# Attention scores issued three head pairs at a time, with one merged exponential behind each projection or feed-forward piece

## The chip, the cores and the metric

The kernel runs on one core of one Trainium2 chip. The metric is the device time of one execution in microseconds; the profile's span runs from the first to the last instruction of the profiled execution. Engines are named as the profile names them: PE (TensorE matmuls), PEld (its weight loads), DVE (VectorE), ACT (ScalarE), POOL (GpSimd), SP (SyncE, whose queue issues the DMAs).

## The reference

A batch of 16 graphs of 1024 nodes with 128 features goes through three graph transformer layers and one graph attention layer; one adjacency matrix (about 1.6% of ones) is shared by all.

```
layer (three times, x of 16 x 1024 x 128, 8 heads of 16):
  Q, K, V = x Wq, x Wk, x Wv
  attn    = softmax over m of (Q K^T / 4, with -inf where adj[n, m] == 0)
  x       = layer_norm(x + attn V Wo + bo)
  x       = layer_norm(x + relu(x W1 + b1) W2 + b2)
last layer (once, one head of 128):
  h   = x W
  e   = leaky_relu(h a_src [i] + h a_dst [j], 0.2), -inf where adj[i, j] == 0
  out = layer_norm(softmax over j of e, times h, plus x)
```

Everything is in float32. The kernel's ordinary path is `fast_path`; `general_path` stands behind a check at the end and isn't run with these inputs.

## The kernel before, in words

The work is cut into 48 blocks, one for each graph and layer, in groups of four graphs (`LANES`): layer 0 of graphs 0 to 3, layer 1 of the same, and so on. A block has 32 attention steps: two groups of four heads (`g`), two halves of 512 queries (`qh`), eight tiles of 128 keys (`kt`). A step has two head pairs (`pp`). In the first and last block the halves are the outer loop. Scores are held transposed: keys on the partitions, queries along the row.

For a head pair, PE makes two score matmuls that share the array by rows (64 rows each; L423) into one PSUM slot of 128 x 1024 from `slot()`. There are three such slots. The pair is then masked in one of two ways. On the DVE way, DVE adds a mask of 0 or a large negative number while it copies the pair to SBUF (L433), and ACT takes the exponential there in place (L445). On the POOL way, ACT takes the exponential on its way out of PSUM (L430), and POOL multiplies by a mask of 0 or 1 (L431). The POOL way is taken by the first pair of a step, except for `kt` in `BOTH_ON_DVE`, so by 5 of 16 pairs. Four steps later (`AHEAD`), `av_due` issues the step's four attention-value products (L450; float32, so eight records in the profile), which share the array by columns and add up in the single PSUM bank `acc`, with the row sums as a seventeenth column. After eight steps the half is finished: `finish` has DVE transpose `acc` to `tt` (L461), and POOL scales it (L464).

The rest of a block's work is cut into pieces held in queues (`chains`). After each step `piece()` takes at most one piece that is due. `proj` pieces make the next block's inputs: two transposes (`t0`), the splits of K and Q into high and low float32r parts (`split`; ACT writes `hi`, L385, DVE writes `lo`, L386), and V. `post` pieces end a block: transposes of the attention result (L477), the output projection, residual addition (L329), layer norm statistics on DVE (L322, L324), `normalise` on POOL (L337 to L341), the feed-forward halves. `last` pieces are the graph attention layer, of which `edges` fills two slots and has DVE turn them into weights (L610), and `aggregate` multiplies these with the nodes. Matmul pieces share the array by columns (L297); transposes take the whole array (L286). Except at both ends of the kernel, all pieces use one PSUM bank, `t`, with one buffer.

When a piece is due is set by a table of steps in its block (`AT`, and `AT_END` near the end) or, for `last`, by distances in steps. The orders of PE and ACT are as written (`manual_schedule`); the orders of DVE, POOL and SP come from a scheduler, in which operations inside `soon()` stand earlier. `stack` copies the split K and Q parts into the row layout of the scores by 32 DMAs from SP for each group of heads. SBUF tiles for exponentials come from `e_tile()`: six buffers of 128 x 4 x 512.

## Time and profile before

| what | value |
|---|---|
| median of 3 runs | 3982.76 us (3978.65 to 3982.88) |
| profiled execution, its own time | 3983.09 us |
| its span | 3981.2 us |
| mean granted PE clock | 0.987 of full speed |
| busy: PE, DVE, ACT, POOL | 3758.5, 3408.3, 3392.8, 3331.4 us |
| HBM traffic | 6 GB/s over the span |

Busy time is that in which at least one instruction of the engine is open. The groups give, for a line and shape, the count, the busy time, the mean duration of one, and the engine's idle time just ahead of it with what ended that. The timeline gives start, duration, engine and line, and merges neighbours of one line ("x4"); a bracket holds idle time and what ended it. The chain follows the work that ended last back through what released each part. Ends of matmuls are modelled, so distances from start to start tell more than durations.

### The profile page before, as it was taken

Reading aid. Unit: us, or ns where it says so; the run is one execution under the profiler, and the core shown is the slowest. Engines: PE = TensorE matmul, PEld = TensorE weight load, DVE = VectorE, ACT = ScalarE, POOL = GpSimd, SP = SyncE. Lnnn points to the kernel's source line nnn. Section 1 sums busy time; section 2 is a strip of 40 time slices with the busy share of each in tenths; the row PEclk is TensorE's granted clock in tenths of the full one; section 3 lists DMA queues with packets and bytes.
Section 4 is the critical chain, followed back from the end, with each engine's and each line's share of the span. In section 5 each row is a group of like instructions: output and inputs, shape, how many; then the busy total and the mean of one; then the engine's idle time right before and its main releaser. Section 6 shows DMA issues by size and latency. Waiting matters only on the chain.

```text
span 3981.2 us, 107823 instructions
## 1 busy us (share of the span) xinstructions
PE 3758.5 (94%) x44501; PEld 1558.5 (39%) x44501; DVE 3408.3 (86%) x5326; ACT 3392.8 (85%) x3961; POOL 3331.4 (84%) x3010
## 2 busy tenths in 40 slices
PE   7999999999999999999999999999999999999996
PEld 2333333344443333334444333333444433333345
DVE  7888988988888988988888898888888898898874
ACT  7999999977779999997777999999777799999860
POOL 4788888987789888988778888888877898898875
PEclk8999999999999999999999999999999999999998
DMA  6222222112222222222222222221222212222200
GB/s 163 65 65 53 55 65 63 46 48 65 56 58 57 65 65 54 54 65 55 55 55 55 65 53 56 65 64 45 55 55 55 71 46 62 65 51 58 66 8 20
DMA packets 124465, 233.13 MB, mean 59 GB/s; under 512 B 34624, under 2 KB 73792, under 8 KB 123968
## 3 DMA queue, kind: packets, MB, share of 16 engines
q1 hardware_dynamic: 123056, 225.74, 22.5%
q8 instruction: 354, 5.80, 0.6%
q14 instruction: 143, 1.17, 0.1%
q10 hardware_dynamic: 912, 0.42, 0.0%
HBM read 15.54 MB, written 8.39 MB: 6 GB/s over the span
## 4 chain that ended last, share of the span: by engine, by line
PE 61%; DVE 22%; POOL 9%; ACT 4%; issue 3%; SPq 0%; DMA 0%; DVEq 0%; ACTq 0%; POOLq 0%
PE acc L450 23%; PE t L297 19%; PE s L423 16%; DVE e L433 13%; POOL e L431 3%; POOL x L341 2%; PE t L286 2%; DVE lo L386 2%; DVE st L322 2%; ACT e L445 2%; ACT e L430 2%; DVE tt L461 1%; POOL mv L339 1%; PE s L297 1%; POOL x L345 1%
## 5 line engine op out<-in xcount | busy, mean ns | idle before, releaser
L433 DVE TENSOR_TENSOR e<-s,mask_add 128x1024 f32<-128x1024 f32 x2112 | 2493.6, 1213 | 344.6 <-PE s L423 263.7
L445 ACT ACTIVATE e<-e 128x1024 f32<-128x1024 f32 x2112 | 2203.4, 1060 | 206.1 <-DVE e L433 187.9
L431 POOL TENSOR_TENSOR e<-e,mask 128x1024 f32<-128x1024 f32 x960 | 1933.5, 2026 | 419.0 <-ACT e L430 419.0
L450 PE MATMUL acc<-e,v 128*17 128x512 f32 x12288 | 1627.8, 601 | 73.3 <-DVE tt L461 47.8
L423 PE MATMUL s<-Wq,Wk 64*128 64x512 f32 x6144 | 1185.0, 456 | 58.1 <-DVE e L433 41.3
L430 ACT ACTIVATE e<-s 128x1024 f32<-128x1024 f32 x960 | 980.8, 1022 | 227.5 <-PE s L423 226.5
L423 PEld LDWEIGHTS s<-Wq,Wk 64*128 64x128 f32 x6144 | 501.2, 185 | 1027.9 <-DVE e L433 417.1
L450 PEld LDWEIGHTS acc<-e,v 128*17 128x17 f32 x12288 | 208.6, 95 | 582.1 <-issue 452.0
L341 POOL TENSOR_SCALAR x<-x,mv 128x128 f32<-128x128 f32 x896 | 389.1, 447 | 23.5
L345 POOL TENSOR_TENSOR x<-x,ln_g 128x1024 f32<-128x1024 f32 (+1 forms) x97 | 229.5, 2367 | 25.1 <-PE t L286 22.6
L339 POOL TENSOR_TENSOR mv<-mv,half_neg 128x4 f32<-128x4 f32 x224 | 232.4, 1038 | 18.6
L297 PE MATMUL t<-hd,e 128*32 128x129 f32 x7040 | 208.2, 275 | 1.2
L329 DVE TENSOR_TENSOR x<-t,x 128x512 f32<-128x512 f32 x191 | 130.8, 685 | 86.9 <-PE t L297 86.9
L297 PEld LDWEIGHTS t<-hd,e 128*32 128x32 f32 x7040 | 194.6, 110 | 16.0 <-issue 5.0
L322 DVE BATCH_NORM_STATS2 st<-x 128x6 f32<-128x128 f32 x896 | 197.3, 280 | 3.3
L297 PE MATMUL t<-x1T,W 128*32 128x512 f32 x1520 | 198.0, 592 | 0.0
L297 PEld LDWEIGHTS t<-W,hT 128*32 128x32 f32 x6080 | 170.0, 110 | 58.5 <-issue 45.5
L297 PE MATMUL t<-W,hT 128*32 128x128 f32 x6080 | 183.4, 273 | 0.2 <-DVE x L625 0.2
L286 PE MATMUL t<-identf,x 128*128 128x128 f32 x872 | 151.0, 289 | 34.0 <-DVE lo L386 15.4
L286 PEld LDWEIGHTS t<-identf,x 128*128 128x128 f32 x872 | 92.9, 141 | 230.2 <-issue 108.3
L337 POOL TENSOR_SCALAR mv<-mv 128x4 f32<-128x4 f32 x224 | 53.0, 236 | 124.6 <-DVE mv L324 98.8
L610 DVE SCALAR_TENSOR_TENSOR e<-s,mask 128x1024 f32<-128x1024 f32 x128 | 150.3, 1214 | 5.9 <-PE s L607 5.0
(118 smaller groups left out, 2573.9 us busy)
## 6 DMA issues: line engine op xcount, KB each, us to landing
Wk<-hi SPq DMA_DIRECT2D x384, 128.0 KB
Wk<-lo SPq DMA_DIRECT2D x384, 128.0 KB
Wq<-hi SPq DMA_DIRECT2D x384, 128.0 KB
Wq<-lo SPq DMA_DIRECT2D x384, 128.0 KB
x<-in_x_dram SPq DMA_DIRECT2D x16, 512.0 KB
out_dram<-x SPq DMA_DIRECT2D x31, 256.0 KB
ai<-in_adj_dram SPq DMA_DIRECT2D x8, 512.0 KB
g_rows<-parts SPq DMA_DIRECT2D x124, 4.0 KB
```

The costliest lines, as they stand in the source:

```text
L286: nc.tensor.transpose(ps[:, t * P:(t + 1) * P], src[:, 4 * h + t, :], identf)
L297: nc.tensor.matmul(dst[j:j + SLOT, :], lhsT[:, j:j + SLOT], rhs, start=start, stop=stop)
L322: nc.vector.bn_stats(st[:, t, :], z[:, t, :])
L339: nc.gpsimd.tensor_tensor(v, v, half_neg[:, ts], OP.pow)
L341: nc.gpsimd.tensor_scalar(z[:, t, :], z[:, t, :], mv[:, t, 0:1], mv[:, t, 1:2], op0=OP.add, op1=OP.mult)
L345: nc.gpsimd.tensor_mul(z, z, rows(gain, n))
L423: nc.tensor.matmul(ps[:, r * 512:(r + 1) * 512], k[64 * r:64 * r + 64, kt * P:(kt + 1) * P], q[64 * r:64 * r + 64, q0:q0 + 512], start=Tru ...
L430: nc.scalar.activation(ev, psv, AF.Exp, scale=HD ** -0.5)
L431: behind["pool"] = nc.gpsimd.tensor_mul(ev, ev, m).ins
L433: behind["dve"] = nc.vector.tensor_add(ev, psv, m).ins
L445: nc.scalar.activation(ev, ev, AF.Exp, scale=HD ** -0.5)
L450: nc.tensor.matmul(acc[j * SLOT:j * SLOT + HD + 1, :], v_bufs[m % 2][:, kt, 2 * j + g, :], e[:, j, :], start=first, stop=last)
```

## The change

Score work is no longer issued by the step but in bursts. A burst is three head pairs in a row (one step and a half), each with its own slot. Its second pair goes the POOL way and the two others the DVE way; every sixteenth burst (`POOL_RESTS`) leaves POOL out. The two DVE pairs of a burst lie side by side in one tile (`e_tile`, five buffers), so that one exponential of 128 x 2048 covers both; the other pair has a tile of its own (`e_pair`, four buffers). The exponential of a burst is issued in the next burst. After the scores of a burst the loop takes one piece if one is due, then issues the exponentials of the burst before, then the attention-value products of the steps that were complete three bursts ago (`AHEAD`), then looks for a piece once more. If two steps are due and the first is the last of its half, that one goes ahead of the piece. The filling of edges becomes a job of its own (`extra`): it takes the place of two pairs in a burst, whose one pair goes the POOL way. The due times lie at multiples of one and a half steps; the K and Q splits alternate; the transposes of the second half come after the first half's feed-forward pieces; `two` now takes its second function first. The last four row blocks of the mask are built in the first four bursts instead of steps 1 to 4.

```diff
-FIRST = 1
-
-
-AT = {"proj": (3, 6, 9, 11, 14, 17, 19, 20), "post": (12, 22, 23, 25, 26, 27, 28, 30, 32, 40, 41)}
-AT_END = {3: (12, 21, 22, 24, 25, 26, 27, 28, 30, 31), 2: (8, 9, 13, 14, 15, 16, 17, 18, 20, 21)}
-AHEAD = 4
-BOTH_ON_DVE = (2, 5, 7)
+
+
+AT = {"proj": (1.5, 4.5, 9, 10.5, 12, 15, 16.5, 18), "post": (13.5, 19.5, 21, 22.5, 24, 25.5, 27, 28.5, 30, 39.5)}
+AT_END = {3: (13.5, 19.5, 21, 22.5, 24, 25.5, 27, 28.5, 30, 31.5), 2: (7.5, 9, 12, 13.5, 15, 16.5, 18, 19.5, 21, 22.5)}
+AHEAD = 3
+BURST = 3
+POOL_RESTS = 16
+E_TILES = {"e": 5, "ep": 4}
...
-        return work.tile([P, J, 512], F32, tag="e", name="e", bufs=6)
+        return work.tile([P, J, 512], F32, tag="e", name="e", bufs=E_TILES["e"])
+
+    def e_pair():
+        return work.tile([P, 2, 512], F32, tag="ep", name="e", bufs=E_TILES["ep"])
...
-        pieces = [t0(0), t0(1), split("Wk", 0), split("Wk", 1), split("Wq", 0), split("Wq", 1), v(0), v(1)]
+        pieces = [t0(0), t0(1), split("Wk", 0), split("Wq", 0), split("Wk", 1), split("Wq", 1), v(0), v(1)]
...
-    def score_step(step):
+    def scores(step, pp):
+
         m, g, qh, kt = step
-        e = e_tile()
-        q0 = qh * 512
-        for pp in range(2):
-            q, k = state["Wq", g, pp], state["Wk", g, pp]
-            ps = slot()
-            for r in range(2):
-                nc.tensor.matmul(ps[:, r * 512:(r + 1) * 512], k[64 * r:64 * r + 64, kt * P:(kt + 1) * P],
-                                 q[64 * r:64 * r + 64, q0:q0 + 512], start=True, stop=True)
-            ev = e[:, 2 * pp:2 * pp + 2, :]
-            psv = ps.rearrange("p (r q) -> p r q", q=512)
-            on_pool = pp == 0 and kt not in BOTH_ON_DVE
-            m = (mask01 if on_pool else mask_add)[:, kt, q0:q0 + 512][:, None, :].to_broadcast([P, 2, 512])
-            if on_pool:
-                nc.scalar.activation(ev, psv, AF.Exp, scale=HD ** -0.5)
-                behind["pool"] = nc.gpsimd.tensor_mul(ev, ev, m).ins
-            else:
-                behind["dve"] = nc.vector.tensor_add(ev, psv, m).ins
-                masked.append((2 * step_no[0] + pp + (kt not in BOTH_ON_DVE), ev))
-        step_no[0] += 1
-        exponentials()
-        return e
-
-    masked, step_no = [], [0]
-
-    def exponentials(n=None):
-
-        while masked and (n is not None or masked[0][0] < 2 * step_no[0] - 1):
-            _, ev = masked.pop(0)
+        q, k = state["Wq", g, pp], state["Wk", g, pp]
+        ps = slot()
+        for r in range(2):
+            nc.tensor.matmul(ps[:, r * 512:(r + 1) * 512], k[64 * r:64 * r + 64, kt * P:(kt + 1) * P],
+                             q[64 * r:64 * r + 64, qh * 512:(qh + 1) * 512], start=True, stop=True)
+        return ps.rearrange("p (r q) -> p r q", q=512)
+
+    def mask_of(mask, step):
+        _, _, qh, kt = step
+        return mask[:, kt, qh * 512:(qh + 1) * 512][:, None, :].to_broadcast([P, 2, 512])
+
+    def on_dve(step, pp, ev):
+        psv = scores(step, pp)
+        behind["dve"] = nc.vector.tensor_add(ev, psv, mask_of(mask_add, step)).ins
+        e_of.setdefault(step, {})[pp] = ev
+
+    def on_pool(step, pp, ev):
+        psv = scores(step, pp)
+        nc.scalar.activation(ev, psv, AF.Exp, scale=HD ** -0.5)
+        behind["pool"] = nc.gpsimd.tensor_mul(ev, ev, mask_of(mask01, step)).ins
+        e_of.setdefault(step, {})[pp] = ev
+
+    e_of, masked, bursts = {}, [], [0]
+
+    def burst(edge, pairs):
+
+        old = list(masked)
+        masked.clear()
+        if edge is not None:
+            edge()
+            on_pool(*pairs[0], e_pair())
+        else:
+            e, ep = e_tile(), e_pair()
+            rests = bursts[0] % POOL_RESTS == POOL_RESTS - 1 or len(pairs) < BURST
+            for i, pair in enumerate(pairs):
+                if i == 1:
+                    (on_dve if rests else on_pool)(*pair, ep)
+                else:
+                    on_dve(*pair, e[:, i:i + 2, :])
+            masked.append(e[:, 0:2 * ((len(pairs) + 1) // 2)])
+            if rests and len(pairs) > 1:
+                masked.append(ep)
+            bursts[0] += 1
+        return old
+
+    def exponentials(evs):
+
+        for ev in evs:
             nc.scalar.activation(ev, ev, AF.Exp, scale=HD ** -0.5)
 
-    def av_step(step, e, acc, first, last):
+    def av_step(step, acc, first, last):
         m, g, qh, kt = step
+        e = e_of.pop(step)
         for j in range(J):
-            nc.tensor.matmul(acc[j * SLOT:j * SLOT + HD + 1, :], v_bufs[m % 2][:, kt, 2 * j + g, :], e[:, j, :],
-                             start=first, stop=last)
+            nc.tensor.matmul(acc[j * SLOT:j * SLOT + HD + 1, :], v_bufs[m % 2][:, kt, 2 * j + g, :],
+                             e[j // 2][:, j % 2, :], start=first, stop=last)
...
-        together = [(5, both, "+w +w"), (1, out_proj(0), "-w"), (1, out_proj(1), "-w"), (5, x1t(0), "+w"), (1, x1t(1), "+w")]
+        together = [(5, both, "+w +w"), (1, out_proj(0), "-w"), (1, out_proj(1), "-w")]
         for h in range(2):
-            together += [(1, ffn1(0, h), "+w"), (1, ffn1(1, h), "+w -w")]
+            together += [(1, x1t(h), "+w"), (1, ffn1(0, h), "+w"), (1, ffn1(1, h), "+w -w")]
...
+    extra = deque()
+
+    def flush():
+        while extra:
+            extra.popleft()()
...
+            def run():
+                extra.append(fill)
+                if tail[0]:
+                    flush()
             return run
...
+                if ("e", u) not in s:
+                    flush()
...
-    def av_due(n):
-
-        for item in [w for w in waiting if w[2] <= n]:
-            step, e, _ = item
-            half = step[:3]
-            if half not in accs:
-                if accs:
-                    continue
-                accs[half] = sums
-                left[half] = NT
-            waiting.remove(item)
-            left[half] -= 1
-            av_step(step, e, accs[half], left[half] == NT - 1, left[half] == 0)
-            if left[half]:
-                continue
+    def av_next():
+
+        step, _ = waiting.popleft()
+        half = step[:3]
+        if half not in left:
+            left[half] = NT
+        left[half] -= 1
+        av_step(step, sums, left[half] == NT - 1, left[half] == 0)
+        if left[half] == 0:
             m, g, qh = half
             b, l = blocks[m]
             while g == 0 and qh == 0 and last_attn:
                 need(last_attn.pop())
-            finish(g, qh, accs.pop(half))()
+            finish(g, qh, sums)()
...
+    late = deque(range(4, NT))
+    full, number = 0, 0
...
+        p = 0
+        while p < 2 * len(steps):
+            edge = extra.popleft() if extra else None
+            take_n = 1 if edge else min(BURST, 2 * len(steps) - p)
+            pairs = []
+            for i in range(p, p + take_n):
+                if i % 2 == 0:
+                    before(i // 2)
+                pairs.append((steps[i // 2], i % 2))
+            if late:
+                with tc.manual_schedule(engines={mybir.EngineType.DVE}):
+                    old = burst(edge, pairs)
+                    t = late.popleft()
+                    neighbours(t)
+                    masks(t, mask_rows(t))
+            else:
+                old = burst(edge, pairs)
+            p += take_n
+            now[0] = p / 2
+            number += 1
+            while full < p // 2:
+                waiting.append((steps[full], number))
+                full += 1
+            if len([w for w in waiting if w[1] <= number - AHEAD]) > 1 and left.get(waiting[0][0][:3]) == 1:
+                av_next()
+            piece()
+            exponentials(old)
+            while waiting and waiting[0][1] <= number - AHEAD:
+                av_next()
+            piece()
+        exponentials(masked)
+        while waiting:
+            now[0] += 1.5
+            for _ in range(min(2, len(waiting))):
+                av_next()
             piece()
```

The function `before`, not shown, holds the same step-bound calls as the old loop (stacking, weights, fetches, new queues), and runs when the first pair of its step is put into a burst. In the new kernel the scores are L428, the DVE add L438, the exponentials L443 and L473, the POOL product L444, and the attention-value products L479.

## Prediction

> **What bounds the kernel now.** I read the page's engine shares first, then the chain that ended last, then the groups by line, then the timeline of TensorE in an undisturbed stretch, and last the waits of TensorE. Shares and chain:
>
> ```profile
> PE 3758.5 (94%) x44501; PEld 1558.5 (39%) x44501; DVE 3408.3 (86%) x5326; ACT 3392.8 (85%) x3961; POOL 3331.4 (84%) x3010
> PE 61%; DVE 22%; POOL 9%; ACT 4%; issue 3%; SPq 0%; DMA 0%; DVEq 0%; ACTq 0%; POOLq 0%
> ```
>
> TensorE leads on the chain and by share, but the other three stand close behind: none has more than 16% of the span free. The costliest groups of each engine:
>
> ```profile
> L433 DVE TENSOR_TENSOR e<-s,mask_add 128x1024 f32<-128x1024 f32 x2112 | 2493.6, 1213 | 344.6 <-PE s L423 263.7
> L445 ACT ACTIVATE e<-e 128x1024 f32<-128x1024 f32 x2112 | 2203.4, 1060 | 206.1 <-DVE e L433 187.9
> L431 POOL TENSOR_TENSOR e<-e,mask 128x1024 f32<-128x1024 f32 x960 | 1933.5, 2026 | 419.0 <-ACT e L430 419.0
> L450 PE MATMUL acc<-e,v 128*17 128x512 f32 x12288 | 1627.8, 601 | 73.3 <-DVE tt L461 47.8
> L423 PE MATMUL s<-Wq,Wk 64*128 64x512 f32 x6144 | 1185.0, 456 | 58.1 <-DVE e L433 41.3
> L430 ACT ACTIVATE e<-s 128x1024 f32<-128x1024 f32 x960 | 980.8, 1022 | 227.5 <-PE s L423 226.5
> ```
>
> TensorE's timeline (start, duration, line) shows what its steps cost; a step runs from the start of one entry to the start of the next:
>
> ```profile
> 2002.70 0.73 PE L423 MATMUL s<-Wq,Wk 64*128 64x512 f32 x4
> 2003.37 1.05 PE L450 MATMUL acc<-e,v 128*17 128x512 f32 x8
> 2004.24 1.04 PE L297 MATMUL t<-x1T,W 128*32 128x512 f32 x8
> 2005.21 0.73 PE L423 MATMUL s<-Wq,Wk 64*128 64x512 f32 x4
> ...
> 2014.27 1.05 PE L450 MATMUL acc<-e,v 128*17 128x512 f32 x8
> 2015.26 0.66 PE L286 MATMUL t<-identf,x 128*128 128x128 f32 x4
> 2015.84 0.73 PE L423 MATMUL s<-Wq,Wk 64*128 64x512 f32 x4
> ...
> 2019.22 0.50 PE L423 MATMUL s<-Wq,Wk 64*128 64x512 f32 x2
> ```
>
> One pair of score matmuls lasts 0.50 us and two 0.73, so a further pair costs about 0.24. Two pairs hold the engine 0.67 us before attention-value work starts: 0.48 of work and 0.19 of changing. Attention-value matmuls (AV, eight records) take 0.87 us when a column-tiled piece follows (2003.37 to 2004.24), but 0.99 ahead of a transpose; a 512-column piece takes 0.97 ahead of scores (2004.24 to 2005.21) against 0.86 when another column-tiled group follows. So leaving that shape costs 0.11.
>
> The sum for TensorE without stalls: 3072 pairs x 0.24 = 737; 1536 AV steps x 0.87 = 1336; 378 pieces of 512 columns x 0.86 = 325; 64 aggregations x 3.68 (from the same timeline, as are the next prices) = 236; 95 second-FFN halves x 1.75 = 166; 189 Wo and Wv halves x 0.89 = 168; transposes, node and edge matmuls about 169. Changes: 1535 score groups x (0.19 + 0.11) = 461, and about 350 other changes x 0.11 = 39. Together 3637. The span is 3981, so about 344 us are stalls, head and tail included. Some are plain on TensorE's waits:
>
> ```profile
> PE acc L450 <- DVE tt L461: 47.8, 84, 1.0
> PE s L423 <- DVE e L433: 41.3, 108, 0.9
> PE acc L450 <- POOL e L431: 16.0, 15, 1.7
> PE t L286 <- DVE lo L386: 15.4, 19, 0.9
> ```
>
> The accumulator is waited for at the end of a half, score slots after DVE, masked pairs after POOL, and the one "t" bank after the previous piece's copy.
>
> [...] scores (64 rows), AV and pieces (32 columns) and transposes (whole array) are three modes, with 0.19 and 0.11 us at their borders and none between AV and a piece. [...] 94% busy holds 500 us of changes. [...]
>
> **The change part by part.** (1) *Bursts.* In the order in which TensorE's instructions are issued, separate score groups fall from 1535 to 1050: about 1000 bursts of three pairs, and some 60 single pairs behind edge matmuls. 485 fewer entries and exits x (0.19 + 0.11) = -145 us. Other changes of mode stay at about 350. No matmul work goes. All of this lies on TensorE, which carries the path: its need falls from 3637 to 3492.
>
> (2) *Merged exponential.* 1006 of 128x2048 and 62 of 128x1024 replace 2112. [...] Off the path while ACT had 15% idle: no direct gain. [...] Slot 1 isn't needed until a burst later.
>
> (3) *Shares of the masks.* POOL takes 998 pairs instead of 960: 38 x 2.026 = +77 us of POOL, -46 of DVE. Hidden so long as AV comes three bursts (about 11 us) behind, against four steps (10.4) before; POOL's longest run between two masks is still about 10 us, so its small waits stay.
>
> (4) *Slots.* Three slots remain. A burst refills all three, so each must be empty one burst later. DVE takes pair 0 at 0.3 us, and pair 2 by 2.7 (its adds start 1.13 apart when back to back); the next burst wants pair 2's slot at about 4.1 (burst of 3.6 us plus 0.5). Slack 1.4, from which come DVE's other operations, about 0.9 a burst on average ((3408 - 2112 x 1.13)/1061 bursts = 1.0), but up to 2.4 where a residual add (0.69), four statistics and four aggregates (1.7) meet. Before, the second pair of a step waited unused for almost two steps, slack 3: here the change tightens. Its price isn't shown: 0 if statistics slip behind adds, 0.7 us in each of the 190 residual bursts (133) at the bad end. I take 40.
>
> (5) *Pieces.* At distances of 1.5 steps the one "t" bank has 3 us rather than 2.5 to clear, and the half's last AV goes ahead of the piece when two AV steps are due, so that the transpose of the accumulator hides behind it. Of the 47.8 + 15.4 us I count 25 back; bounds 0 and 60.
>
> (6) *Edges.* 64 edge pieces become bursts with one pair; their DVE operations (2 x 1.21) are those of before. An extra tile in the five- and four-deep rotation may hold one exponential until AV: 0 to 1.5 us in 30 bursts, so 0 to 45; I take 10. SP's DMAs are the same number in nearly the same order; the head's four row blocks now share four bursts; both zero, plus or minus 10.
>
> Sum: 3981 - 145 + 40 - 25 + 10 = 3861; with DVE and POOL now at 87 to 90% of a shorter span I return another 10 for queueing, hence **3871**, 3873 with the 1.9 us around the span. The profiled execution (3983.1) is 0.3 above the median, so **3872** is compared with 3982.8. My own range for this case is 3800 to 3940.
>
> **Rivals.** *More is gained:* [...] 3871 less 100, about 3765. For it: TensorE's listed waits are on copies and accumulators that the order relieves. Against: a shorter period leaves DVE and POOL less slack. *The saving is eaten:* four engines within 10% of each other are the bound; as TensorE speeds up it only waits longer for DVE's slots, and the 145 come back as waits: 3980. For it: the chain already has 22% on DVE. Against: DVE has 573 us free. *Slower, by the third slot:* DVE reaches pair 2 only after a residual add that itself waits for the piece, and TensorE[...] stands before the third pair with AV and piece queued behind it. The break-even is 145/1061 = 0.14 us more stall per burst; if each of the 190 residual bursts and the 190 that take a transposed accumulator loses 0.65, that is +247, so 4083. For it: the slack of 1.4 against 2.4 of other work. Against: the add that follows gets its time back in lighter bursts. *The change doesn't do what it says* isn't likely: the issue order shows six score matmuls in a row.
>
> **How the numbers follow.** Main case 0.52; more 0.14; eaten 0.08, spread evenly about no change; slower 0.26. About 0.2% (8 us) is what a measurement of this kernel can tell from no change. Faster 0.67, same 0.06, slower 0.27. The range 3765 to 4070 leaves out about half of the "more" case and the far third of the slower one.
>
> **What would show it.** Right: L423's successor sees score groups of x6 with about 1.1 us before AV starts; TensorE busy falls by some 100 to 150 us; waits of TensorE and its loads on DVE's adds stay near their present total[...]. Step 4 is wrong if waits for the score slots grow by over 100 us; step 5 if the wait for tt stays at 48. The forecast is wrong if score groups are broken by waits inside[...].

## The result: slower by 2.8%, and the profile after

The changed kernel takes 4092.4 us (median of four, 4091.1 to 4102.0) against 3982.8 us of the kernel before measured beside it: a ratio of 1.028, 95% interval 1.0261 to 1.0299. The profiled execution has a span of 4091.3 us, 110.1 more than before. The forecast was 3872, and the sign was wrong too.

The page after, busy shares and the chain that ended last:

```profile
PE 3695.3 (90%) x44501; PEld 1620.2 (40%) x44501; DVE 3335.9 (82%) x5288; ACT 3285.3 (80%) x2955; POOL 3403.7 (83%) x3048
...
PE 42%; DVE 36%; POOL 10%; issue 5%; ACT 4%; SPq 1%; DMA 0%; DVEq 0%; ACTq 0%; POOLq 0%
```

TensorE is busy for 63 us less, so it did get something; but its idle time (span less busy) rose from 222.7 to 396.0 us, by 173. The share of every engine but the weight loads fell, and on the chain DVE's part grew from 22% to 36%, while TensorE's fell from 61% to 42%. The groups (busy time and mean of one; then idle time ahead and what ended it):

```profile
L438 DVE TENSOR_TENSOR e<-s,mask_add 128x1024 f32<-128x1024 f32 x2074 | 2423.4, 1211 | 386.5 <-PE s L428 370.0
L444 POOL TENSOR_TENSOR e<-e,mask 128x1024 f32<-128x1024 f32 x998 | 2008.6, 2026 | 397.7 <-ACT e L443 388.2
L473 ACT ACTIVATE e<-e 128x2048 f32<-128x2048 f32 x1068 | 1989.8, 1873 | 1.3 <-DVE e L438 1.3
L479 PE MATMUL acc<-e,v 128*17 128x512 f32 x12288 | 1545.7, 601 | 62.8 <-DVE tt L490 48.8
L428 PE MATMUL s<-Wq,Wk 64*128 64x512 f32 x6144 | 1096.2, 443 | 169.6 <-DVE e L438 96.5
L443 ACT ACTIVATE e<-s 128x1024 f32<-128x1024 f32 x998 | 1027.2, 1029 | 420.1 <-PE s L428 346.6
```

No instruction became dearer to speak of: the DVE add is 1211 ns (1213 before), the POOL product 2026 as before, the first-pass exponential 1029 (1022). (L473 mixes 1006 exponentials of full width with 62 of half width.) What grew most is TensorE's idle time in front of the scores, from 58.1 to 169.6 us. In front of the pieces that write the bank "t" it grew too, from 45 to 97 us, added up over all their groups; these two make up 163 of the 173 us. TensorE's timeline (start, duration, line; in brackets idle time and what ended it) shows where it stands:

```profile
1400.09 0.96 PE L428 MATMUL s<-Wq,Wk 64*128 64x512 f32 x6
1400.98 1.05 PE L479 MATMUL acc<-e,v 128*17 128x512 f32 x8
1401.98 0.73 PE L428 MATMUL s<-Wq,Wk 64*128 64x512 f32 x4
1403.11 0.50 PE L428 MATMUL s<-Wq,Wk 64*128 64x512 f32 x2 [0.40 <-DVE e L438]
1403.54 1.05 PE L479 MATMUL acc<-e,v 128*17 128x512 f32 x8
...
1451.04 0.96 PE L428 MATMUL s<-Wq,Wk 64*128 64x512 f32 x6
1451.93 1.06 PE L304 MATMUL t<-x1T,W 128*32 128x512 f32 x8
```

The burst at 1451.04 is whole: six score matmuls, 0.89 us to the next entry. The one at 1401.98 is broken before its third pair. The burst ahead of it began only 1.89 us earlier, since one AV step and no piece stood between them, while DVE needs two adds of 1.21, so 2.4 us, to empty the first and third slot.

This is the usual case. I measured the distances from the start of one burst to the start of the next in one stretch of the timeline, 1345 to 1630 us (about a group of four layer-1 blocks), and counted which of the later bursts came in parts, with a wait of over 0.15 us inside. The last two columns count the same for all bursts of three pairs in the whole span:

| distance from the burst before | bursts in the stretch | of them broken | bursts in the span | of them broken |
|---|---|---|---|---|
| under 2.3 us | 7 | 7 | 105 | 95 |
| 2.3 to 3.2 us | 35 | 9 | 342 | 74 |
| over 3.2 us | 41 | 1 | 548 | 19 |

Most of these waits end with a DVE add (L438), some with the exponential of the second pair (ACT, L443). One kind of burst stands out: 58 bursts of the span follow one of the sixteenth bursts, in which DVE has three adds and not two. Of these, 39 are broken, all 36 that come within 3.2 us among them, and they hold 46 of the 130 us that TensorE waits inside bursts.

The waits, of TensorE's weight loads, of DVE and of TensorE (total, times, longest):

```profile
PEld s L428 <- DVE e L438: 562.4, 726, 2.7
...
DVE col L664 <- PE t L304: 148.7, 50, 5.6
...
PE s L428 <- DVE e L438: 96.5, 166, 2.1
...
PE acc L479 <- DVE tt L490: 48.8, 50, 2.2
...
PE s L428 <- DVE e L645: 27.5, 36, 1.4
```

Before, the first of these rows was

```profile
PEld s L423 <- DVE e L433: 417.1, 542, 1.7
```

and the third stood at 41.3 us: together 200 us more of TensorE and its loads waiting for DVE's adds. The loads' waits lie partly beside matmuls (the 562.4 us of the first row alone are more than TensorE's whole idle time of 396.0), so this sum isn't lost time; it is still 644 us in e12_pool below, which is almost as fast as the kernel before. The idle time before the scores says more. The wait for the accumulator's transpose is where it was (47.8).

**By stage.** The accumulator transposes on DVE (L461 before, L490 after) mark the end of each half; every sixteenth ends a group of four blocks. From their starts come the lengths of the stages: the head (layer 0 of graphs 0 to 3), the four plain groups (layer 1), the four groups of layer 2, the three groups of layer 0 that carry the last layer of the graphs before, and the tail behind the last half. In us, with the median of each run:

| kernel | median | head | layer 1 | layer 2 | layer 0 | tail |
|---|---|---|---|---|---|---|
| before | 3982.8 | 330 | 1170 | 1295 | 1089 | 97 |
| after | 4092.4 | 340 | 1166 | 1321 | 1137 | 128 |
| e1_tail | 4069.5 | 341 | 1165 | 1320 | 1143 | 103 |
| e8_avfwd | 4049.9 | 339 | 1166 | 1312 | 1124 | 103 |
| e12_pool | 3996.7 | 335 | 1143 | 1299 | 1117 | 105 |
| e16_splitagg | 4057.2 | 333 | 1143 | 1317 | 1169 | 92 |
| e3_split | 4180.9 | 344 | 1206 | 1356 | 1149 | 126 |
| e4_burst2 | 4128.6 | 335 | 1187 | 1373 | 1118 | 115 |
| e10_avhalf | 4153.7 | 342 | 1208 | 1349 | 1143 | 106 |

The 110 us are therefore made up of four things: 31 in the tail, 74 in the stages of layers 2 and 0, 10 in the head, and a plain stage that gained 4 where its share of the 145 us (four of twelve groups) would have been 48.

### The profile page after: what moved, and what is told of

Read it like the earlier page. It is cut to its first block, busy times and chain, and to the rows that moved or that the text cites. A ratio compares the mean times of both kernels' runs of the same rounds, so it can differ in the third digit from the quotient of the medians.

```text
span 4091.3 us, 106755 instructions
## 1 busy us (share of the span) xinstructions
PE 3695.3 (90%) x44501; PEld 1620.2 (40%) x44501; DVE 3335.9 (82%) x5288; ACT 3285.3 (80%) x2955; POOL 3403.7 (83%) x3048
## 4 chain that ended last, share of the span: by engine, by line
PE 42%; DVE 36%; POOL 10%; issue 5%; ACT 4%; SPq 1%; DMA 0%; DVEq 0%; ACTq 0%; POOLq 0%
DVE e L438 21%; PE acc L479 15%; PE t L304 14%; PE s L428 9%; POOL e L444 4%; DVE st L329 3%; DVE e L645 2%; DVE x L336 2%; POOL x L352 2%; ACT e L473 2%; PE t L293 2%; POOL x L353 2%; DVE lo L393 2%; DVE tt L490 2%; ACT e L443 1%
## 5 line engine op out<-in xcount | busy, mean ns | idle before, releaser
L438 DVE TENSOR_TENSOR e<-s,mask_add 128x1024 f32<-128x1024 f32 x2074 | 2423.4, 1211 | 386.5 <-PE s L428 370.0
L444 POOL TENSOR_TENSOR e<-e,mask 128x1024 f32<-128x1024 f32 x998 | 2008.6, 2026 | 397.7 <-ACT e L443 388.2
L473 ACT ACTIVATE e<-e 128x2048 f32<-128x2048 f32 x1068 | 1989.8, 1873 | 1.3 <-DVE e L438 1.3
L479 PE MATMUL acc<-e,v 128*17 128x512 f32 x12288 | 1545.7, 601 | 62.8 <-DVE tt L490 48.8
L443 ACT ACTIVATE e<-s 128x1024 f32<-128x1024 f32 x998 | 1027.2, 1029 | 420.1 <-PE s L428 346.6
L428 PE MATMUL s<-Wq,Wk 64*128 64x512 f32 x6144 | 1096.2, 443 | 169.6 <-DVE e L438 96.5
L428 PEld LDWEIGHTS s<-Wq,Wk 64*128 64x128 f32 x6144 | 512.4, 185 | 1142.4 <-DVE e L438 562.4
L479 PEld LDWEIGHTS acc<-e,v 128*17 128x17 f32 x12288 | 315.5, 98 | 690.8 <-issue 602.8
L352 POOL TENSOR_TENSOR x<-x,ln_g 128x1024 f32<-128x1024 f32 x97 | 229.5, 2366 | 51.9 <-PE t L293 47.0
L329 DVE BATCH_NORM_STATS2 st<-x 128x6 f32<-128x128 f32 x896 | 196.8, 279 | 4.1
L535 ACT ACTIVATE hT<-t,b 128x512 f32<-128x512 f32 x190 | 132.5, 697 | 43.9 <-PE t L304 43.8
L392 ACT CAST hi<-t 128x512 fp32r<-128x512 f32 x188 | 110.3, 587 | 63.4 <-PE t L304 62.2
```

The lines of the kernel that those rows point to most:

```text
L329: nc.vector.bn_stats(st[:, t, :], z[:, t, :])
L352: nc.gpsimd.tensor_mul(z, z, rows(gain, n))
L428: nc.tensor.matmul(ps[:, r * 512:(r + 1) * 512], k[64 * r:64 * r + 64, kt * P:(kt + 1) * P], q[64 * r:64 * r + 64, qh * 512:(qh + 1) * 512 ...
L438: behind["dve"] = nc.vector.tensor_add(ev, psv, mask_of(mask_add, step)).ins
L443: nc.scalar.activation(ev, psv, AF.Exp, scale=HD ** -0.5)
L444: behind["pool"] = nc.gpsimd.tensor_mul(ev, ev, mask_of(mask01, step)).ins
```

## The experiments

Two theories stood at first. One: the score slots, held by DVE in bursts that follow each other too closely, eat the saving, and the tail's order and the edge bursts add to it. The rival: the loss is made by the order of the pieces and exponentials, by ACT or by the waits for "t" and the accumulator. In the diffs, - is the changed kernel and + the experiment, unless another kernel is named. All times are medians; ratios are to the kernel before.

### The tail and the edges

**e1_tail.** With the `two` of the kernel before in the tail, so that the edges of the next rows are begun before the aggregation of the last:

```diff
             def run():
-                g()
-                f()
+                if tail[0]:
+                    f()
+                    g()
+                else:
+                    g()
+                    f()
```

> The changed kernel with one thing put back: behind the last scores, where pieces run alone, `two` fills the edges of the next 256 nodes ahead of the aggregation, as before; elsewhere it stays as changed. Theory E (the loss lies in how edges are placed): the tail behind the last half took 128 us after and 97 before, since each aggregation now waits for edges that are only begun when the one ahead of it is done (about 2 x 1.13 us of DVE and 0.7 of PE, eight times); expected 4092 less 25 to 31, so 4061 to 4067. Theory S (the loss lies in the three slots that a burst refills at once): the tail's 31 us have another cause[...], and the time stays above 4082.

Measured 4069.5 us, ratio 1.0223 (1.0206 to 1.024); the tail falls from 128 to 103 us, and no other stage moves by more than 6. Three lines of the timeline of the changed kernel's tail, and the corresponding ones of the kernel before:

```profile
4034.34 0.73 PE L642 MATMUL s<-g_rows,h_rows 4*128 4x256 f32 x8
4036.94 0.66 PE L304 MATMUL s<-hd,e 128*32 128x129 f32 x8 [1.87 <-DVE e L645]
4038.14 4.59 PE L304 MATMUL s<-hd,e 128*32 128x129 f32 x120 [0.54 <-DVE e L645]
```

```profile
3947.29 0.73 PE L607 MATMUL s<-g_rows,h_rows 4*128 4x256 f32 x8
3948.39 7.30 PE L297 MATMUL s<-hd,e 128*32 128x129 f32 x256 [0.36 <-DVE x L625]
```

After the change an aggregation waits 1.87 and 0.54 us for the edges that were issued just ahead of it; before, two aggregations ran without a gap, since their edges had been made during the aggregation before. The swapped order cost 23 us, by the medians, and the prediction had no term for it.

**e2_edges.** e1_tail, with the edges filled at once instead of in the place of two pairs of a burst:

```diff
-                extra.append(fill)
-                if tail[0]:
-                    flush()
+                fill()
```

> As e1_tail, and the edges are filled inside their piece again, not as a job that takes the place of two pairs in a burst. Theory E: the 75 us that the stages with edges lost (layers 2 and 0) come back too, so about 3985 (3970 to 4005), and those stages fall to 320 and 363 us for four blocks or below. Theory S: bursts of three lose in every stage, edges or not; no more than 20 us beyond e1_tail come back, so 4040 to 4065.

Measured 4161.3 us, ratio 1.046 (1.0438 to 1.0481): 92 us more than e1_tail. Both theories had expected a gain. An edge's tile now also comes at another place in the five-deep rotation, so slots and tiles change together and the loss has no single cause. It shows only that, in this loop, edges in place of two pairs are the better of the two.

**e8_avfwd.** e1_tail, with the AV step due one burst earlier when a burst holds an edge and one pair, so that TensorE has work while DVE empties the edge's two slots:

```diff
-            while waiting and waiting[0][1] <= number - AHEAD:
+            while waiting and waiting[0][1] <= number - AHEAD + (1 if edge else 0):
```

> As e1_tail (4069), and a burst that holds edges and one pair takes the attention-value products of one more burst, so that TensorE has 0.9 to 1.7 us more of other work before the next three slots are wanted. If the lost time of layers 2 and 0 lies in the next burst's wait for the slots of the edges (seen as 0.7 to 1.3 us twice behind an edge group), up to 64 x 1 us come back: 4005 to 4045. If they lose by the long aggregations or by DVE's total work: above 4060.

Measured 4049.9 us, ratio 1.0171 (1.0154 to 1.0188): 20 less than e1_tail. In the changed kernel an edge's burst looks like this:

```profile
2079.98 0.74 PE L642 MATMUL s<-g_rows,h_rows 4*128 4x256 f32 x8
2080.66 0.50 PE L428 MATMUL s<-Wq,Wk 64*128 64x512 f32 x2
2082.00 0.83 PE L428 MATMUL s<-Wq,Wk 64*128 64x512 f32 x4 [0.85 <-DVE e L645]
2084.17 0.50 PE L428 MATMUL s<-Wq,Wk 64*128 64x512 f32 x2 [1.33 <-DVE e L645]
2084.60 1.93 PE L304 MATMUL t<-xT,Wk 128*32 128x512 f32 x8
```

Nothing lies between the edge's pair at 2080.66 and the next burst, which then waits twice for DVE's edge operations, 2.2 us in all. In e8_avfwd the row of TensorE's score matmuls waiting for these falls from 27.5 us to 2.0. In layers 2 and 0 it gives back 8 and 19 of e1_tail's time.

**e11_agglate and e13_agglate.** DVE waits 148.7 us at the aggregation's reciprocal (`col`, L664), where score adds may queue behind it. Here aggregations are taken only behind the AV steps, on e8_avfwd and on e1_tail:

```diff
-            if is_due(chain) and take(chain):
+            if is_due(chain) and (long or not hasattr(chain["queue"][0][1], "long")) and take(chain):
...
-            piece()
+            piece(False)
             exponentials(old)
```

The first place for a piece, directly behind the scores, now refuses aggregations.

> As e8_avfwd (4050), and the aggregations (3.7 us on TensorE) are taken behind the attention-value products of their burst, never directly behind the scores. Theory G (a long piece between scores and attention-value products starves DVE, which stands at the aggregation's reciprocal with its adds done, 149 us of waits against 50 before): layers 2 and 0 fall by 20 to 40 in all, 4005 to 4030. Theory S (only the distance from one burst to the next counts, and that is unchanged): 4040 to 4060.

> As e1_tail (4069), without e8_avfwd's moved products, with the aggregations behind the attention-value products. Theory G: 4030 to 4055, and with e11_agglate it shows whether the two edits add up. Theory S: 4060 to 4078.

Measured 4062.1 us (1.0212, 1.0195 to 1.0229) and 4078.4 us (1.0247, 1.023 to 1.0264): 12 and 9 us more than their bases. Taking the aggregations later in their burst doesn't help.

### DVE and the slots

**a_light and b_light.** Both kernels leave out three of every four layer-norm statistics on DVE (L329 after, L322 before); all four row tiles use those of the first:

```diff
-        for t in range(ts.start, ts.stop):
-            nc.vector.bn_stats(st[:, t, :], z[:, t, :])
+        nc.vector.bn_stats(st[:, ts.start, :], z[:, ts.start, :])
...
```

> The changed kernel with the layer norm's statistics taken from the first of every four row tiles only (one BATCH_NORM_STATS2 instead of four; the other three tiles use it too), so the normalisation is of the wrong rows for three quarters. It takes 672 operations of about 0.21 us start to start from DVE, 140 us, and nothing from the other engines. Theory S (between bursts TensorE waits for DVE, in every stage): it gives back most of what a busy DVE costs, 60 to 120 us: 3970 to 4030, and in the plain stages (layer 1) more than the kernel before gains from the same cut. Theory T (the due times and the place of the pieces cost, DVE being free 18% of the time): below 40 us, 4050 to 4092.

> The kernel before with the same cut of statistics (one of every four row tiles, used for all four). By theory S its two slack slots hide DVE better, so it gains less than the changed kernel does: 0 to 40 us, 3940 to 3980. By theory T both gain alike.

The changed kernel falls to 4041.2 us (1.0148, 1.0131 to 1.0165), the kernel before to 3972.8 (0.9973, 0.9962 to 0.9984). DVE's busy time fell by 103 us in the one and by 123 in the other. So a microsecond of this work of DVE is worth 51/103 = 0.5 us after the change and 10/123 = 0.08 before it: the change put DVE on the path. TensorE's idle time before its scores falls from 169.6 to 127.9 us in a_light, which is most of the 51.

**e12_pool.** e8_avfwd, with no burst leaving POOL out. Every sixteenth burst had three adds on DVE, 3.6 us of work in a mean period of about as much:

```diff
-POOL_RESTS = 16
+POOL_RESTS = 100000
```

> As e8_avfwd (4050), and no burst leaves POOL out: 63 pairs more on POOL (+128 us), 63 fewer on DVE (-70), 63 fewer single exponentials after the add. The changed kernel gained 0.5 us for each us of DVE taken away, so by theory S -35: 4010 to 4030. If POOL (83% busy, with runs of 10 us between masks) binds as much as DVE, the time rises: 4060 to 4100.

Measured 3996.7 us, ratio 1.0037 (1.0023 to 1.0051): 53 us less than e8_avfwd for 62 adds moved, 0.86 us for an add of 1.21. The busy line of e12_pool, and its scores beside those of e8_avfwd (first row):

```profile
PE 3647.8 (91%) x44501; PEld 1602.1 (40%) x44501; DVE 3269.7 (82%) x5226; ACT 3287.6 (82%) x2955; POOL 3523.9 (88%) x3110
```

```profile
L428 PE MATMUL s<-Wq,Wk 64*128 64x512 f32 x6144 | 1095.5, 443 | 152.9 <-DVE e L438 114.6 <-ACT e L443 11.5 <-DMA Wk<-hi 7.4
L428 PE MATMUL s<-Wq,Wk 64*128 64x512 f32 x6144 | 1085.1, 442 | 99.7 <-DVE e L438 77.9 <-DMA Wq<-lo 6.1 <-ACT mask_add L216 3.9
```

TensorE's idle time before its scores falls by 53 us as well. The edit also takes 62 separate exponentials of 1024 columns from behind the merged ones, but of the 53 us only 8 are waits for ACT and 37 are waits for DVE's adds. The bursts in the places behind those with three adds hold 9 us of waits where the changed kernel has 46. Bursts within 2.3 us of the one before are still mostly broken (92 of 111), for 38 us in all. So what this run gives back was lost mainly behind the bursts of three adds, and not by short distances alone.

DVE is 67 us less busy, POOL 119 more, at 88%. The plain stage falls from 1166 to 1143 us, so that 27 of its 48 us are now there. It is the best version found, and still 0.4% slower than the kernel before.

**e14_pool16 and e15_pool8.** e12_pool, where every sixteenth, or every eighth, burst gives its third pair to POOL as well:

```diff
+            both = bursts[0] % 16 == 8          # e15_pool8: bursts[0] % 8 == 4
...
+                elif i == 2 and both:
+                    on_pool(*pair, e[:, 2:4, :])
...
-            masked.append(e[:, 0:2 * ((len(pairs) + 1) // 2)])
+            masked.append(e[:, 0:2] if both else e[:, 0:2 * ((len(pairs) + 1) // 2)])
```

> As e12_pool (3997), and the third pair of every sixteenth burst goes to POOL too: some 63 pairs more on POOL (+128 us, then about 3650 us busy), 63 fewer DVE adds, each of them the one that holds the third slot. Theory S: -20 to -50, 3945 to 3975, which would beat the kernel before. If POOL at 88% is by now the next bound: 3990 to 4040.

> As e14_pool16 with every eighth burst: 126 pairs more on POOL than e12_pool (+255 us, about 3780 us busy of some 3970), 126 fewer DVE adds. POOL must bind before this pays: slower than e14_pool16 by 20 us or more; if it is faster, DVE alone holds the third slot and POOL has more room than its share says.

Measured 4043.1 us (1.0149, 1.0132 to 1.0166) and 4147.5 us (1.0408, 1.0391 to 1.0425): 46 and 151 more than e12_pool. The busy line and the chain of e15_pool8:

```profile
PE 3701.1 (89%) x44501; PEld 1615.6 (39%) x44501; DVE 3140.0 (76%) x5100; ACT 3299.1 (80%) x3081; POOL 3767.3 (91%) x3236
...
POOL 46%; PE 27%; DVE 17%; issue 4%; ACT 3%; SPq 1%; DMA 0%; DVEq 0%; POOLq 0%; ACTq 0%
```

POOL leads the chain with 46%. POOL is no cheaper place for further adds: in e12_pool it is already busy for 88% of the span, and a product takes 2.03 us there against 1.21 on DVE.

**e10_avhalf.** e1_tail, with single AV steps split by 256 query columns, so that a burst is followed by some one and a half steps rather than one or two:

```diff
+            if steps_due == 1 and waiting and waiting[0][1] <= number - AHEAD + 1 and waiting[0][0][3] and not edge:
+                begun.add(waiting[0][0])
+                av_step(waiting[0][0], sums, False, False, 0)
...
```

> As e1_tail (4069), with a step of attention-value products split by query columns where a burst would get one step, so that bursts get about 1.5 steps each instead of one and two in turn; the work is the same but for some 430 x 8 further short matmuls. Bursts without a piece then last 2.3 us on TensorE instead of 1.9 and 2.8. Theory S (a short burst catches DVE unready, and the time isn't made up): the plain stages fall from about 291 to 283 to 287 us for four blocks and the whole by 30 to 60, to 4010 to 4040. If unevenness between bursts is absorbed: within 15 us of 4069.

Measured 4153.7 us, ratio 1.0431 (1.0414 to 1.0449): 84 more than e1_tail. In a stretch of plain work (1350 to 1640 us) no burst follows within 2.3 us, but 45 lie at 2.3 to 3.2 us and 12 of them are broken; over the span TensorE's idle time before its scores is 206.4 us, against 168.4 in e1_tail. This goes against the forecast of theory S. Evening the distances doesn't pay in this form; it issues 3464 more matmul records, and TensorE's busy time rises from 3692.6 to 3715.8 us.

### Exponentials, pieces and the burst itself

**e3_split.** The changed kernel with each merged exponential issued as two of 128 x 1024:

```diff
         for ev in evs:
-            nc.scalar.activation(ev, ev, AF.Exp, scale=HD ** -0.5)
+            for i in range(0, ev.shape[1], 2):
+                nc.scalar.activation(ev[:, i:i + 2], ev[:, i:i + 2], AF.Exp, scale=HD ** -0.5)
```

> The changed kernel with the merged exponential issued as two of 128x1024 again, in the same place. ACT had 20% idle, so if merging is off the path the time rises by 0 to 15 us (4092 to 4107). If ACT's delay of the next burst's exponential (1.9 us in one piece) is part of the loss, splitting changes nothing of that, since both halves stand in the same place; a fall below 4080 would speak for a wait on the whole of the merged tile by the attention-value products, a rise over 30 us for ACT being near the path.

Measured 4180.9 us, ratio 1.0505 (1.0487 to 1.0522): 89 more than the changed kernel. The busy line, the chain and the exponential of e3_split:

```profile
PE 3745.9 (90%) x44501; PEld 1646.5 (39%) x44501; DVE 3338.9 (80%) x5288; ACT 3367.9 (81%) x3961; POOL 3405.3 (81%) x3048
...
PE 38%; DVE 30%; ACT 15%; POOL 9%; issue 5%; SPq 1%; DMA 1%; DVEq 0%; ACTq 0%; POOLq 0%
...
L474 ACT ACTIVATE e<-e 128x1024 f32<-128x1024 f32 x2074 | 2084.6, 1069 | 0.0
```

ACT gets only 83 us busier, and the time rises by 89. With 20% idle, ACT is nevertheless near the path: its share of the chain goes from 4% to 15%. By my reading that is because copies and first-pass exponentials, on which slots and pieces depend, stand behind it: the waits for the first-pass exponential rise from 19.8 to 31.9 us for the scores and from 92.9 to 123.9 us for their weight loads.

**e4_burst2.** The new loop with bursts of two pairs, a lead of four bursts, unmerged exponentials, and the kernel before's share of POOL:

```diff
-AHEAD = 3
-BURST = 3
-E_TILES = {"e": 5, "ep": 4}
+AHEAD = 4
+BURST = 2
+E_TILES = {"e": 2, "ep": 10}
...
-            e, ep = e_tile(), e_pair()
-            rests = bursts[0] % POOL_RESTS == POOL_RESTS - 1 or len(pairs) < BURST
+            e, ep = e_pair(), e_pair()
+            rests = bursts[0] % 8 in (2, 5, 7) or len(pairs) < BURST
...
```

> The changed kernel with bursts of two pairs (one step), everything else of the new loop kept: edges as a job of their own, piece directly behind the scores, the same due times. The exponential is then 1024 wide, POOL takes 5 of 8 second pairs, attention-value products come four bursts behind. Theory S: two pairs leave one slot free, so waits for score slots fall and the time drops by 100 or more, below 3990, though the mode changes come back (+145 us of TensorE need). Theory E: the edges' place is unchanged, and the mode changes come back; 4090 or above.

Measured 4128.6 us, ratio 1.0373 (1.0356 to 1.039). TensorE's waits in it:

```profile
PE s L428 <- DVE e L438: 28.7, 80, 0.6
```

The wait of the scores for DVE's adds is below its 41.3 us of the kernel before, so the slots are no longer short. By theory S the time should then have fallen below 3990 us; it is 36 above the changed kernel and 146 above the kernel before. So the slots are not the whole loss. What the new loop costs with two pairs shows in the pieces: TensorE's idle time before those that write "t" is 140 us here against 45 in the kernel before, and it is busy for 52 us more. Whether the place of the piece or the due times (which lie at multiples of one and a half steps, and a burst here is one step) do this isn't told apart.

The neighbour of this run with three pairs and unmerged exponentials is e3_split. TensorE is busy for 3810.8 us here and 3745.9 there, although the granted clock is lower there (0.965 against 0.983): with fewer changes of mode it is busy for 65 us less. But e3_split is 52 us slower, and its wait in the same row is 121.0 us. As far as two kernels that also differ in tiles and in POOL's share can tell, three pairs without the merging lose.

**e5_tables and e9_oldtables.** The new due times and orders on the kernel before, and the old ones on the changed kernel:

```diff
-AT = {"proj": (3, 6, 9, 11, 14, 17, 19, 20), "post": (12, 22, 23, 25, 26, 27, 28, 30, 32, 40, 41)}
+AT = {"proj": (1.5, 4.5, 9, 10.5, 12, 15, 16.5, 18), "post": (13.5, 19.5, 21, 22.5, 24, 25.5, 27, 28.5, 30, 39.5)}
...
```

This is e5_tables, against the kernel before; e9_oldtables does the reverse.

> The kernel before with the new due times alone: the tables, the alternating K and Q splits, and the transpose of the second half behind the first half's feed-forward pieces. If the new order of pieces is part of the loss, the stages with attention of the last layer (layers 2 and 0) lengthen by 20 us or more in all and the time is 4000 to 4030. If it is neutral or good, as forecast (25 us fewer waits on the t bank and the accumulator), 3955 to 3985.

> The changed kernel with the old due times and the old order of pieces (tables, K and Q splits, both transposes of the second half first). On the old loop the new times alone cost 53 us. If they are simply worse, the old ones give that back here: 4020 to 4060. If they were chosen for bursts (a piece in each), the old ones bunch two pieces into one burst and leave others without: above 4110.

Measured 4035.7 us (1.0135, 1.0119 to 1.0152), 53 more than the kernel before; and 4206.3 us (1.0557, 1.0539 to 1.0575), 114 more than the changed kernel. Each table fits its own loop. The wait of TensorE for the accumulator's transpose does answer to them: on the old loop it falls from 47.8 to 26.4 us, and on the new one it is 90.3 with the old tables and 48.8 with the new. So the relief is real, but the new loop uses it up, and on the old one more is lost elsewhere than comes back. There the scores now wait for the first-pass exponential, which cost 0.7 us before:

```profile
PE s L423 <- ACT e L430: 42.0, 102, 0.6
```

**e6_expfirst and e7_piecelast.** The exponentials ahead of the piece, and both places for a piece behind exponentials and AV:

```diff
+            exponentials(old)
             piece()
-            exponentials(old)
```

```diff
-            piece()
             exponentials(old)
             while waiting and waiting[0][1] <= number - AHEAD:
                 av_next()
+            piece()
             piece()
```

> The changed kernel with the exponentials of the last burst issued ahead of the burst's piece on ACT, TensorE's order the same. Theory A (ACT is near the path because it stands still before the piece's copy while an exponential is ready; splitting the exponential cost 89 us): ACT saves the wait, but the piece's copy comes up to 1.9 us later and the next piece waits for the t bank. If the standstill rules, the time falls by 20 to 60, to 4030 to 4070; if the late copies rule, it rises, 4110 to 4160. Theory S (DVE and the three slots alone): within 15 us of 4092.

> The changed kernel with its pieces behind the attention-value products, not directly behind the scores; ACT then has the exponential ahead of the copies. If a long piece (an aggregation, 3.7 us) right behind the scores is what starves DVE and ACT, nothing changes here, since it stands between the same two bursts: within 20 us of 4092. If the piece's place matters through its copy, the copy now comes just ahead of the next burst and holds the next burst's exponential and slot: 4120 to 4200.

Measured 4419.5 us (1.1098, 1.108 to 1.1117) and 4409.8 us (1.1065, 1.1046 to 1.1083): 327 and 317 more than the changed kernel. One row of the waits of e6_expfirst, and one group of e7_piecelast:

```profile
PE t L304 <- DVE lo L393: 143.0, 104, 3.2
```

```profile
L479 PE MATMUL acc<-e,v 128*17 128x512 f32 x12288 | 1607.6, 623 | 91.5 <-DVE tt L490 88.4
```

Both lie far above every forecast. With a merged exponential ahead of it, the copy of the "t" bank comes late and TensorE stands before the next piece: 143.0 us against 22.6 in the changed kernel. In e7_piecelast it stands longer for the transposed accumulator, 88.4 us against 48.8, and for the same copies, 77.6. So the changed kernel's place for the piece, directly behind the scores and ahead of the exponential, is the better one in this loop.

**e16_splitagg.** e12_pool, with each aggregation cut into two pieces of one row tile. The timeline had shown it as one block of 3.7 us:

```diff
-                for i in range(2):
-                    for t in range(NT):
-                        by_columns(ps[:, i * (D + 1):(i + 1) * (D + 1)], e[:, t, i * P:(i + 1) * P],
+                for t in range(NT):
+                    by_columns(ps[:, :D + 1], e[:, t, i * P:(i + 1) * P],
...
-                (3, two(edges(2), aggregate(1)), ""), (3, two(edges(3), aggregate(2)), ""),
+                (3, aggregate(1, 0), ""), (1.5, two(edges(2), aggregate(1, 1)), ""),
```

> The version of the run before that lets no burst leave POOL out, the tail in its old order and the attention-value products of edge bursts one burst earlier (3996.7 us), with each aggregation of the last layer cut into two pieces of one row tile each, at distances of 3 and 1.5 steps. An aggregation of two row tiles stands between two score bursts for some 3.7 us. If these long bursts cause what is still lost in the stages with the last layer (about 35 us against the kernel before), the time falls to 3960 to 3985 us. If the slots of the edge bursts cause it, or the fixed number of bursts, the time stays at 3990 to 4020 us, since eight further pieces a graph bring small operations to DVE.

Measured 4057.2 us, ratio 1.0191 (1.0172 to 1.0209): 60 more than e12_pool. One row of its waits:

```profile
DVE col L663 <- PE t L304: 108.3, 61, 4.5
```

DVE's wait at the reciprocal did fall, from 158.4 in e12_pool, and the plain stage is the same to a microsecond; but layer 0 takes 52 and layer 2 18 us more. Shorter aggregations and less standing of DVE behind them don't bring the loss of these stages back; as the split adds pieces of its own, it doesn't clear the length of the aggregation either. That the further pieces find too few places between bursts would fit the numbers, but isn't shown.

## Why the prediction was wrong

The forecast had 145 us less work on TensorE and 35 us more waiting (40 for slots, 25 back at the pieces, 10 for edges, 10 for queueing). The profile has 63 us less busy time and 173 more idle time. The miss of 220 us is thus 82 us of busy time and 138 of waiting. The step that failed is step 4, followed by step 5; most of what is missing in step 1 can be put down to the waits that these two left out.

**Step 1, the changes of mode: right in their price.** A burst of six takes 0.89 us to the next entry, against 0.67 + 0.24 = 0.91 by the prediction's own prices (the 1.1 us among its signs doesn't follow from them); an AV step ahead of scores takes 1.00 (1400.98 to 1401.98) against 0.87 + 0.11 = 0.98. TensorE's busy time fell only by 63 us instead of 100 to 150. Two estimates bring this near the 145. A broken burst is longer besides its wait (1401.98 to 1403.54 is 1.56, less 0.40 is 1.16 against 0.89), which for 166 waits is 0.27 x 166 = 45 us, if all are like this one. And the mean granted clock fell from 0.987 to 0.976, which over the two spans is (0.024 x 4091) - (0.013 x 3981) = 46 us of lost clock. In e12_pool, where the clock is back at 0.985 and the waits inside bursts are shorter, the busy time is 111 us below that of the kernel before, within the forecast.

**Step 4, the third slot: the step that failed.** It took 40 us for a tightening whose own bounds were 0 and 133; TensorE's idle time before its scores rose by 112. Two premises were wrong. It let every burst last the mean of 3.6 us, so that the third slot would be wanted at 4.1; the table of distances shows about half of the bursts nearer than 3.2, and those nearer than 2.3 nearly all broken, though it takes no residual addition for that. And it spread DVE's adds evenly, though every sixteenth burst has three: taking these away is worth 53 us (e12_pool). By the prediction's own mark (slot waits up by over 100 us) it fell: they rose by 200. The rival *slower, by the third slot* had the right slot and sign, for the wrong bursts: it charged the residual bursts, and it had a chance of 0.26. That its 4083 us lies so near the measured time is partly luck, since it held neither the tail nor the edges nor the pieces.

**Step 2, the merged exponential: cheaper, but not off the path.** The 1006 exponentials of full width take 1924 ns each, where two of 1024 columns took 2 x 1060 = 2120 before, and the two groups of exponentials lost 167 us between them (2203.4 + 980.8 before, 1989.8 + 1027.2 after). ACT as a whole fell by 107.5 only, to 3285.3: its other groups grew by 11, and instructions of different groups overlap by 49 less (all groups add up to 303 us more than the engine's busy time before, to 254 more after). "No direct gain" fails: undone, it costs 89 us. "Off the path while ACT had 15% idle" was read from a share; the share said nothing of how many copies and slot releases queue behind ACT.

```profile
L473 ACT ACTIVATE e<-e 128x2048 f32<-128x2048 f32 x1006 | 1931.2, 1924 | 1.3 <-DVE e L438 1.3
```

**Step 5, the pieces: wrong.** 25 us were to come back; the wait for the accumulator stayed at 48.8, the mark set for this, and TensorE's idle time before the pieces that write "t" rose from 45 to 97 us. The new due times and orders bring no gain of their own (53 us lost on the old loop); they only fit the new one. That the new loop with two pairs (e4_burst2) loses 146 us points the same way.

**Step 6, the edges, and what no step held.** 10 us were taken for tiles. The edge burst's slots cost about 20 (e8_avfwd against e1_tail), and the order of `two` in the tail 23, which stood in the diff and was given no price. The head cost 10, the edge of its "zero, plus or minus 10".

**Step 3** holds as far as the profile tells: TensorE's 16.0 us of waits for masked pairs of POOL are gone, and POOL's idle time ahead of the products fell only by 21. POOL had room for 62 pairs more (e12_pool), but not for a further 63 (e14_pool16).

Together: 110 us, of which 23 are the tail's order, 20 the edge bursts, 53 the bursts of three adds; they bring 3996.7. There layers 2 and 0 still take 32 us more than before, and the tail and head 13, while the plain stage gains 27. Where this stands can be read: in the stages of layers 2 and 0, TensorE's idle time before its scores is 29 us above that of the kernel before, and before the pieces that write "t" 65 us above (40 before, 105 in e12_pool). So most of what remains are waits for the one "t" bank, of which the scores' bursts are one possible cause and the new places and times of the pieces another; no run parts them. Late aggregations, split aggregations and evened AV steps don't bring it back.

## What to carry to other kernels

Grouping work to save changes of mode also groups the demand for the buffers it fills. Compare the distances between groups, the short ones and not only their mean, with the time that the consumer needs to empty the buffers, and price the consumer's work per group, the heaviest group first: here 62 bursts with three adds, of over a thousand, were worth 53 us. A producer that waits inside a group also delays the other work that stands behind it (the AV step behind the broken burst of 1401.98 began 1.56 us after the burst's start, behind a whole one the next entry began after 0.89), so look at the waits for every buffer, not only for the one that was regrouped. A diff's small reversals, such as the order of two functions, need a line in the sum each; the tail shows them undiluted.

## What the runs showed of the hardware

In one place a short stall was followed by half the clock. Two rows of the changed kernel's view by windows (window, length, busy time and number of instructions of TensorE, its loads, DVE, ACT and POOL; then granted clock, DMA share, GB/s), for the edge burst shown above:

```profile
2082.00:2084.60 2.60, 1.27 (x7) 0.56 (x7) 2.60 (x10) 2.08 (x2) 2.15 (x2) 0.99 0.00 0
2084.60:2086.60 2.00, 2.00 (x14) 0.54 (x16) 1.77 (x2) 0.00 (x0) 1.74 (x4) 0.50 0.03 8
```

TensorE was busy for 1.27 of 2.60 us at a clock of 0.99, and in the next window its clock is 0.50: the piece at 2084.60 took 1.93 us where the one at 1451.93 takes 1.06. From 2072.84 to 2084.60 us no wait was longer than 1.33 us. The wait of 1.79 us that ends at 2071.28 wasn't followed by such a fall: from 2072 to 2082 us the clock is 1.00. That the stall brought the lower clock isn't shown. Over the whole span:

```profile
core 0: 4091.3 us, clock 0.976
```

The kernel before has 0.987 and e12_pool 0.985; e6_expfirst and e7_piecelast, in which TensorE is idle for 649 and 633 us, have 0.957 and 0.956.
